# A Mamba block, attention and a mixture of experts on one core: dense products in TensorE's waits behind the scans, and the last queries as three tiles and one

## The chip, the core and the metric

The kernel runs on one core of one Trainium2 chip. A core has five engines that run side by side, each through its own queue in order: TensorE (PE in the profile; its weight loads are PEld) multiplies matrices into PSUM, VectorE (DVE) and ScalarE (ACT) work on tiles, GpSimd (POOL) does a few small operations and here issues the indirect transfers, and SyncE (SP) issues most of the DMA. They wait for each other by semaphores. The metric is the time of one execution on the device, in microseconds (us); the median of several runs counts. In the profile a matmul is shown with the clock that TensorE was granted (PEclk, 1.00 is full speed).

## What is computed

The input is `x` of 4 sequences of 1024 tokens with 128 channels, in float32. Two layers follow each other, each with a residual and a layer norm behind it.

```
# layer 1: a selective state space model, 256 inner channels, 16 states
xz = x @ in_proj_w.T ; xb, z = halves of xz
xb = silu(causal_conv(xb, 4 taps)) ; proj = xb @ x_proj_w.T   # dt_in, B (16), C (16)
dt = softplus(dt_in * dt_w + dt_b)
h[t] = exp(dt[t] * A) * h[t-1] + xb[t] * dt[t] * B[t]         # a scan over 1024 tokens
y = sum over states of h * C + xb * D_param
x = layernorm(x + (layernorm(y) * silu(z)) @ out_w.T)

# layer 2: causal attention (16 heads of 8), then 16 experts, two for each token
n1 = layer_norm(x) ; q, k, v = n1 @ q_w, n1 @ k_w, n1 @ v_w
hidden = x + softmax(causal(q k^T / sqrt(8))) v @ o_w
xt = layer_norm(hidden) ; logits = xt @ router_w
top1, top2 = the two largest ; slot = running count of the expert's tokens before this one
# a token whose slot is beyond the expert's capacity of 512 is dropped for that expert
moe = sum over both experts of gate * 0.8 * fc2(gelu(fc1(xt)))
x = layernorm(x + hidden + moe)
```

A token's place in its expert is a running count over all tokens before it (`cumsum` over the 4096 tokens), so the routing of the last tokens needs the totals of all earlier ones.

## The kernel before

Tokens are worked on in 32 tiles of 128; half a sequence is 512 tokens, four tiles. The program has three stages. First the scans of layer 1 run, half a sequence at a time; VectorE is their engine. Beside them, and behind them for the last sequence, runs attention. Then come the experts: each reads its 512 slots (`xe`, L1462), runs two products and a GELU, and scatters its rows to the tokens (L1492). At the end the two rows of each token are added with their gates.

Attention works on one half sequence of queries at a time (`stream`, L756), in four groups of four heads (`for g in range(NG)`). For each block of 128 keys it makes scores (`pst`, L782), their exponentials on ScalarE (`pr`, L792), and weighted sums (`av`, L804) one block later. Blocks on the diagonal are masked; for the very last half (`e.last`) VectorE does so by a product with a triangle (L795). A group's sums end in `avs` (L843).

The order of the queues of TensorE and VectorE is that of the program text (`manual_schedule` with `pinned` engines), and that text is interleaved by hand: each side task is a generator, cut by `yield` into pieces, and `piece()` (L1566) advances each of its queues by one piece for every key block of attention (`next(attend)`). A `yield USE` marks a piece whose results are used in the first round of the next call, ahead of the scores. The queues are `before` (inputs of the next half: norm, transposes, products of queries and keys, L669), `after` and `final` (what follows a half's weighted sums), `aside` (routing), `loads` (expert weights) and `sending` (transfers of routed rows).

What follows weighted sums: for all halves but the last `rest_of_half` (L854) divides by the sums of the exponentials, which go through DRAM, and projects (L886); `tokens_of_half` (L931) transposes back; `after_projection` (L942) adds the residual, norms the rows (L960), transposes them (L969) and makes the logits (L975) and their copy in `lg` (L980). For the last half `group_of_last` (L890) does it group by group: a product with a selector spreads the sums (L911), a reciprocal and a product on VectorE (L916, L917), the projection (L923) into one bank that all groups add to. Its fourth group is done in two halves of two tiles each (L811 to L845), so that the norm of the first two lies beside the scores of the others; the second goes to `final`.

The norm behind the scans (`pace.first`) takes its inverse root by three Newton steps on VectorE (`inv_std_steps`, L156), four small operations a step.

Routing (`send`, L1259) takes a range of tiles: the largest logit, its place by products with a triangle into `pcum` (L1333), slots, then the same for the second; then each tile's two rows go out by indirect DMA on GpSimd (`transfer`, L1279). Tiles 0 to 15, 16 to 23 and 24 to 27 are sent while attention runs, one transfer after the other; each waits for the one before. The last four tiles are routed when the loop has ended (L1687), and their eight transfers follow each other without such waits. The experts' reads wait for the last group of transfers (`sent[-1]`, L1463). `counted` (L1613) counts the halves that are through, by which the ranges become due (L1682 to L1685).

Of the kernel before, what the change touches and what calls it, by code (L numbers as in the profile page):

```python
# [10 lines left out]
F32 = mybir.dt.float32  # L11
# [3 lines left out]
ALU = mybir.AluOpType  # L15
# [32 lines left out]
NPART, NPAIR = 3, 9  # L48
USE = 1
SCORE_MAX = 40.0  # L50


@with_exitstack
def mamba_then_moe_block_kernel(ctx: ExitStack, tc: tile.TileContext, a: dict, out: bass.AP):
# [101 lines left out]
    def inv_std_steps(pool, var, n, tag):  # L156


        ve = pool.tile([P, n], F32, tag=tag + "_ve", name=tag + "_ve")
        nc.vector.tensor_scalar(ve, var, LN_EPS, None, ALU.add)  # L160
        r = pool.tile([P, n], F32, tag=tag + "_rs", name=tag + "_rs")
        t = pool.tile([P, n], F32, tag=tag + "_nt", name=tag + "_nt")
        nc.vector.tensor_scalar(r.bitcast(I32), ve.bitcast(I32), 1, None, ALU.logical_shift_right)
        nc.vector.tensor_scalar(r.bitcast(I32), r.bitcast(I32), -1.0, float(0x5F3759DF), ALU.mult, ALU.add)
        for _ in range(3):
            nc.vector.tensor_tensor(t, r, r, ALU.mult)
            nc.vector.tensor_tensor(t, t, ve, ALU.mult)
            nc.vector.tensor_scalar(t, t, -0.5, 1.5, ALU.mult, ALU.add)
            nc.vector.tensor_tensor(r, r, t, ALU.mult)
        return r  # L170
# [486 lines left out]
    def attention(ph, weights, last_bank):  # L657
# [98 lines left out]
        def stream(todo, then, rows, after, final):  # L756
# [3 lines left out]
            while True:  # L760
# [8 lines left out]
                for g in range(NG):  # L769
# [40 lines left out]

                    halves = 2 if e.last and g == NG - 1 else 1  # L811
                    n = TPH // halves
                    for i0 in range(0, TPH, n):
                        nkb = TPH * qt + i0 + n
# [29 lines left out]
                        if e.last:  # L844
                            then(group_of_last(e, g, t, rows, i0, n), i0 + n == TPH and g == NG - 1, final if i0 else after)  # L845
                    if not e.last:
                        nc.sync.dma_start(e.sums[4 * g : 4 * g + 4, :], t[HD : P : 32, :])
                if not e.last:
                    then(rest_of_half(e, avs, rows), True)
                todo.popleft()  # L850

        held, HELD = [], 5
# [37 lines left out]
        def group_of_last(e, g, t, rows, i0, n):  # L890
# [28 lines left out]
            if not i0:  # L919
                yield  # L920
            po = zbank("po") if i0 else e.po
            for i in range(i0, i0 + n):
                nc.tensor.matmul(  # L923
                    po[:, i * P : (i + 1) * P], lhsT=t[:, i * P : (i + 1) * P], rhs=wo[:, g, :],
                    start=i0 > 0, stop=i0 > 0 or g == NG - 1 and i == i0 + n - 1,
                )
            if g == NG - 1:
                yield USE
                yield from after_projection(e, po, rows, i0, n, e.hid if i0 else None)
# [12 lines left out]
        def after_projection(e, pt, rows, i0, n, hid=None):  # L942
# [20 lines left out]
            if rows.xrow is None:  # L963
                to_tokens(x2_d, t0, x2)
                rows.stored = t0 + 4
            yield
            pt = zbank("pt_x2")
            for i in range(n):
# [14 lines left out]

        return inputs, stream

# [213 lines left out]
    def routing(ph):  # L1199
# [45 lines left out]

        totals, sent, in_turn = [None, None], [], []

# [10 lines left out]

        def send(t0, n, bank, later=None, staged=False):  # L1259
            ts = slice(t0, t0 + n)  # L1260
# [12 lines left out]

            group = (f"sent{t0}", []) if later is None else None
            earlier = in_turn[-1:]
            if group:
                sent.append(group[1])

            def transfer(i, t, row):  # L1279
                ins = scatter(xin, s.put[i][:, t : t + 1], row, group, earlier)  # L1280
                if group:
                    wait_for(ins, earlier)
                else:
                    in_turn[:] = [ins]
# [37 lines left out]
            def places(m, i, name):  # L1322
# [18 lines left out]
                nc.vector.tensor_reduce(place, loc, AX.X, ALU.add)  # L1341
                total = keep.tile([P, E], F32, tag=f"total{i}_{t0}", name=f"total{i}")
                if totals[i] is None:
# [210 lines left out]
    with tc.If(mild > 0) as cmp:  # L1554

        with ExitStack() as late:
            with ExitStack() as ph:
# [54 lines left out]

                def counted(rest):  # L1613
                    yield from rest
                    finished.append(rest)
                    if len(finished) * TPH == SOON:
                        after.append(send(0, SOON, bank_z, sending.append, staged=True))
# [10 lines left out]
                with ExitStack() as ssm:  # L1628
                    with ExitStack() as first:
# [15 lines left out]
                    last_bank = lambda name: ps_last.tile([P, HL], F32, tag="last", name=name)  # L1645
                    attention_inputs, attention_stream = attention(ph, weights, last_bank)
                    attend = attention_stream(
                        middle, lambda rest, all_, to=after: to.append(counted(rest) if all_ else rest), rows, after, final
                    )
# [18 lines left out]
                def send_early(t0, n):  # L1668
# [122 lines left out]
```

## Time and profile before

| | us |
|---|---|
| three runs | 1239.41, 1233.44, 1253.04 (median 1239.41) |
| the profiled execution | 1231.83, its span 1229.9 |
| mean granted clock of TensorE | 0.848 |
| busy: TensorE, VectorE, ScalarE, GpSimd | 923.8, 880.8, 678.4, 265.2 |
| last weighted sums of the half before the last | 893.5 |
| first scores of the last half | 901.66 |
| routing of the last four tiles | 1032.3 to 1039.5 |
| their transfers on GpSimd | 1036.6 to 1046.4 |
| first expert's transposes | 1050.90 |
| first expert's result on VectorE | 1062.84 |

A line of the timeline has the start, the time that a run of like instructions took, the engine, the line of the program, what it writes from what, the shape, how many, and in brackets how long the engine had stood idle and what ended that. A line of the windows has, for a stretch of time, its length and for each engine the busy time with the number of instructions, then the granted clock, the DMA engines' busy share and GB/s. A busy TensorE in the profile is one with a product in flight; it need not be at its peak. One product of float32 shows as two records.

### The profile page before, as it was taken

Reading aid. Unit: us, or ns where it says so; the run is one execution under the profiler, and the core shown is the slowest. Engines: PE = TensorE matmul, PEld = TensorE weight load, DVE = VectorE, ACT = ScalarE, POOL = GpSimd, SP = SyncE. Lnnn points to the kernel's source line nnn. Section 1 sums busy time; section 2 is a strip of 40 time slices with the busy share of each in tenths; the row PEclk is TensorE's granted clock in tenths of the full one; section 3 lists DMA queues with packets and bytes.
Section 4 is the critical chain, followed back from the end, with each engine's and each line's share of the span. In section 5 each row is a group of like instructions: output and inputs, shape, how many; then the busy total and the mean of one; then the engine's idle time right before and its main releaser. Section 6 shows DMA issues by size and latency. Waiting matters only on the chain. (4 is left out here: it accounts for less than half of the span.)

```text
span 1229.9 us, 15466 instructions
## 1 busy us (share of the span) xinstructions
PE 923.8 (75%) x5388; PEld 442.2 (36%) x5388; DVE 880.8 (72%) x1328; ACT 678.4 (55%) x1006; POOL 265.2 (22%) x248
## 2 busy tenths in 40 slices
PE   4687852267889888889988497987878873789965
PEld 2332310033434334424334233332422332566645
DVE  2199698999899999899999999788543555112205
ACT  1467556235787894577875366575443551823224
POOL 1020012130211001101102213454103202244443
PEclk9989976566999998799989688888956995899997
DMA  3965476616554553542562442133662201522117
GB/s 69 308 245 198 158 268 224 217 65 219 164 172 132 171 163 127 159 144 82 194 181 72 160 149 88 44 115 110 155 191 89 74 12 52 170 67 69 46 36 206
DMA packets 170680, 171.02 MB, mean 139 GB/s; under 512 B 31984, under 2 KB 126144, under 8 KB 170464
## 3 DMA queue, kind: packets, MB, share of 16 engines
q1 hardware_dynamic: 155296, 143.16, 38.5%
q10 hardware_dynamic: 11200, 18.35, 4.1%
q0 software_dynamic: 4096, 8.43, 2.1%
q8 instruction: 44, 0.72, 0.3%
q14 instruction: 44, 0.36, 0.1%
HBM read 110.80 MB, written 59.10 MB: 138 GB/s over the span
## 5 line engine op out<-in xcount | busy, mean ns | idle before, releaser
L792 ACT ACTIVATE pr<-pst 128x1024 f32<-128x1024 f32 (+3 forms) x396 | 292.9, 792 | 121.2 <-PE pst L782 72.0
L536 ACT ACTIVATE da<-dt_sp,a_neg 128x512 f32<-128x512 f32 x256 | 179.0, 722 | 117.9 <-DVE h L542 106.8
L782 PE MATMUL pst<-qst,kst 72*128 72x512 bf16 (+3 forms) x792 | 197.1, 351 | 41.3 <-ACT pr L792 19.9
L804 PE MATMUL av<-pr,vp 128*32 128x512 f32 (+3 forms) x1584 | 181.3, 526 | 2.0 <-DVE pr L795 1.6
L532 DVE TENSOR_TENSOR h<-u_sp,bt 128x2048 f32<-128x2048 f32 x64 | 145.4, 2276 | 16.5 <-DMA u_sp<-u_d 16.5
L542 DVE TENSOR_TENSOR_SCAN h<-da,carry,h 128x512 f32<-128x512 f32 x128 | 155.8, 1265 | 1.7 <-ACT da L536 1.7
L542 DVE TENSOR_TENSOR_SCAN h<-da,h 128x512 f32<-128x512 f32 x128 | 148.4, 1206 | 6.7 <-ACT da L536 6.7
L552 PE MATMUL py<-h,sel 128*32 128x512 f32 x512 | 86.9, 758 | 83.8 <-DVE h L548 55.0
L548 DVE TENSOR_TENSOR h<-h,ct 128x2048 f32<-128x2048 f32 x64 | 146.2, 2285 | 1.1 <-POOL carry L545 0.3
L782 PEld LDWEIGHTS <-kst 72*128 72x128 bf16 x792 | 66.3, 103 | 183.0 <-issue 153.5
L545 POOL COPY carry<-h 128x4 f32<-128x4 f32 x32 | 44.6, 1392 | 355.6 <-DVE h L542 336.9
L1477 ACT ACTIVATE hT<-ph,b 128x512 f32<-128x512 f32 x64 | 43.9, 686 | 80.7 <-PE ph L1476 79.7
L127 POOL DMA_INDIRECT eout<-eo,to x64 | 61.4, 960 | 88.4 <-DVE eo L1488 54.1
L301 PE MATMUL pt_x<-xT,w_tap 128*128 128x512 f32 x128 | 60.8, 631 | 18.2 <-DVE w_tap L283 7.4
L1476 PE MATMUL ph<-xeT,w 128*128 128x512 f32 x128 | 61.9, 619 | 12.9 <-DVE xeT L1472 12.9
L1483 PEld LDWEIGHTS po_e<-w,hT 128*128 128x128 f32 x512 | 61.5, 192 | 13.0 <-issue 12.2
L127 POOL DMA_INDIRECT xin<-row,put x32 | 47.0, 1468 | 77.1 <-issue 29.3
L1483 PE MATMUL po_e<-w,hT 128*128 128x128 f32 x512 | 63.2, 277 | 0.1
L788 PE MATMUL pst<-mask_k,identb 128*128 128x128 bf16 x448 | 62.8, 225 | 0.0
L127 POOL DMA_INDIRECT xin<-xrow,put x32 | 31.1, 971 | 137.5 <-DVE p L1211 45.3
L804 PEld LDWEIGHTS av<-pr,vp 128*32 128x32 f32 x1584 | 36.3, 112 | 60.8 <-issue 37.6
L552 PEld LDWEIGHTS py<-h,sel 128*32 128x32 f32 x512 | 12.3, 119 | 123.4 <-DVE h L548 69.1
(255 smaller groups left out, 1200.5 us busy)
## 6 DMA issues: line engine op xcount, KB each, us to landing
dt_sp<-dt_d SPq DMA_DIRECT2D x64, 256.0 KB
u_sp<-u_d SPq DMA_DIRECT2D x64, 256.0 KB
kst<-k_parts SPq DMA_DIRECT2D x96, 144.0 KB
qst<-q_parts SPq DMA_DIRECT2D x64, 144.0 KB
bt<-bc_d SPq DMA_DIRECT2D x32, 256.0 KB
ct<-bc_d SPq DMA_DIRECT2D x32, 256.0 KB
w<-in_fc_w_dram SPq DMA_DIRECT2D x32, 256.0 KB
xin<-clear SPq DMA_DIRECT2D x8, 516.0 KB
```

The lines of the kernel that those rows point to most:

```text
L127: ins = nc.gpsimd.indirect_dma_start(out=dst[:, :], out_offset=bass.IndirectOffsetOnAxis(ap=rows, axis=0), in_=src, in_offset=None).ins
L532: nc.vector.tensor_tensor(s.h, s.u, four(s.bt), ALU.mult)
L536: nc.scalar.activation(s.da[jl], s.dt[:, jl, :], AF.Exp, scale=a_neg[:, j, s.g : s.g + 1])
L542: ins = nc.vector.tensor_tensor_scan(h, s.da[jl], h, from_, ALU.mult, ALU.add).ins
L548: nc.vector.tensor_tensor(s.h, s.h, four(s.ct), ALU.mult)
L552: nc.tensor.matmul(s.py[jl * NR : (jl + 1) * NR, :], lhsT=sel, rhs=s.h[:, jl, :], start=(s.g == 0), stop=(s.g == NG_S - 1),)
L782: nc.tensor.matmul(pst[:, jj, :w], lhsT=ks[ki // TPH][jp][:, jj, ki % TPH * P : (ki % TPH + 1) * P], rhs=qs[jp][:, jj, q0:c1], start=True, ...
L788: nc.tensor.matmul(pst[:, jj, :P], lhsT=identb, rhs=mask_k, start=False, stop=True)
L792: nc.scalar.activation(pr[:, :, :w], pst[:, :, :w], AF.Exp, scale=QSCALE)
L804: nc.tensor.matmul(av[32 * j : 32 * j + 32, q0 : q0 + w], lhsT=e.vps[ki // TPH][:, ki % TPH, v0 : v0 + 32], rhs=pr[:, jj, :w], start=(ki = ...
L1476: nc.tensor.matmul(phh, lhsT=w1[e][:, c * P : (c + 1) * P], rhs=xeT, start=True, stop=True)
L1483: nc.tensor.matmul(po[:, i, :], lhsT=hT[:, c, i * P : (i + 1) * P], rhs=w2[e][:, c, :], start=(c == 0), stop=(c == NFC - 1),)
```

## The change

It has six parts. (1) A new function `busy(n)` issues `n` products of the identity with itself, 128x512 in float32, into one of the two banks of the scores; nobody reads them. It is called with 7 ahead of the first group of the last half, with 3 and 6 before and behind the last projection of the last tile, and with 2, 1, 2, 2 and 12 behind the pieces of the last routing. (2) The fourth group of the last half is split into three tiles and one, for two and two. (3) `group_of_last` has one more `yield` ahead of the projection, and `after_projection` three more between the norm and the transposes, when the scans are over. (4) A Newton step is three operations for four. (5) `counted` counts tiles, not halves, so the first three tiles of the last half are routed as a range of their own, and the last tile as another; the three tiles' transfers are a group whose members do not wait for each other, and the last tile's two wait for all of that group. (6) The running totals alternate between two buffers for each choice, for one buffer per range.

```diff
+BUSY, BUSY_SUMS, BUSY_NORM = 7, 3, 6
+BUSY_SEND = 2, 1, 2, 2, 12
...
         for _ in range(3):
             nc.vector.tensor_tensor(t, r, r, ALU.mult)
-            nc.vector.tensor_tensor(t, t, ve, ALU.mult)
-            nc.vector.tensor_scalar(t, t, -0.5, 1.5, ALU.mult, ALU.add)
-            nc.vector.tensor_tensor(r, r, t, ALU.mult)
+            nc.vector.scalar_tensor_tensor(t, t, -0.5, ve, ALU.mult, ALU.mult)
+            nc.vector.scalar_tensor_tensor(r, t, 1.5, r, ALU.add, ALU.mult)
...
-                    halves = 2 if e.last and g == NG - 1 else 1
-                    n = TPH // halves
-                    for i0 in range(0, TPH, n):
+                    if e.last and g == 0:
+                        busy(BUSY)
+                    for i0, n in ((0, TPH - 1), (TPH - 1, 1)) if e.last and g == NG - 1 else ((0, TPH),):
...
-                            then(group_of_last(e, g, t, rows, i0, n), i0 + n == TPH and g == NG - 1, final if i0 else after)
+                            then(group_of_last(e, g, t, rows, i0, n), n if g == NG - 1 else 0, final if i0 else after)
...
-                    then(rest_of_half(e, avs, rows), True)
+                    then(rest_of_half(e, avs, rows), TPH)
...
+        def busy(n):
+            pst = ps_s.tile([P, 2, HL], F32, tag="ps_s", name="pst_busy")
+            for i in range(n):
+                nc.tensor.matmul(
+                    pst[:, i % 2, :], lhsT=ident, rhs=ident.unsqueeze(1).to_broadcast([P, HL // P, P]),
+                    start=True, stop=True,
+                )
...
             if not i0:
                 yield
+                yield
+            else:
+                busy(BUSY_SUMS)
             po = zbank("po") if i0 else e.po
             for i in range(i0, i0 + n):
...
+            if i0:
+                busy(BUSY_NORM)
             if g == NG - 1:
                 yield USE
...
             yield
+            if pace.first and not i0:
+                for _ in range(3):
+                    yield
             pt = zbank("pt_x2")
...
-            group = (f"sent{t0}", []) if later is None else None
-            earlier = in_turn[-1:]
+            group = (f"sent{t0}", []) if later is None or free else None
...
             def transfer(i, t, row):
+                earlier = sent[-2] if len(sent) > 1 and later is None else in_turn[-1:]
                 ins = scatter(xin, s.put[i][:, t : t + 1], row, group, earlier)
...
-                total = keep.tile([P, E], F32, tag=f"total{i}_{t0}", name=f"total{i}")
+                tag = f"total{i}_{ranges[i] % 2}"
+                ranges[i] += 1
+                total = keep.tile([P, E], F32, tag=tag, name=f"total{i}")
...
-                def counted(rest):
+                def counted(rest, n):
                     yield from rest
-                    finished.append(rest)
-                    if len(finished) * TPH == SOON:
+                    if not n:
+                        return
+                    finished.append(n)
+                    if sum(finished) == SOON:
...
-                    yield from send(t0, n, bank, sending.append)
+                    last = t0 + n > NT - TPH
+                    yield from send(t0, n, bank_z if last else bank, sending.append, free=last)
...
-                        known = len(finished) * TPH
+                        known = sum(finished)
...
-                for _ in send(early, NT - early, bank):
-                    pass
+                for i, _ in enumerate(send(early, NT - early, bank)):
+                    busy(BUSY_SEND[i])
```

With it the order on TensorE becomes: the transposes and logits of the half before the last behind the last products of queries and keys, then the seven products, then group 0; the transposes and logits of the next half at the sixth and seventh key block of group 1; the products of group 0 (L907, L911, L923) in group 2, together with the routing of tiles 24 to 27; the logits of the three tiles behind the last weighted sums, then the last tile's, then the routing of the three tiles, then that of the last tile, then 14 products ahead of the first expert.

More of the change, by code (lines that the diff above doesn't have):

```diff
@@ L982, in after_projection @@
             )
-        return inputs, stream
+        return inputs, stream, busy
     def attention_with_maxima(ph):
@@ L1244, in rows_of @@
             return s.xrow, s.behind
-        totals, sent, in_turn = [None, None], [], []
+        totals, ranges, sent, in_turn = [None, None], [0, 0], [], []
         def has_slot(t0, n):
@@ L1257, in has_slot, with send @@
             return ok
-        def send(t0, n, bank, later=None, staged=False):
+        def send(t0, n, bank, later=None, staged=False, free=False):
             ts = slice(t0, t0 + n)
@@ L1645, in mamba_then_moe_block_kernel @@
                     last_bank = lambda name: ps_last.tile([P, HL], F32, tag="last", name=name)
-                    attention_inputs, attention_stream = attention(ph, weights, last_bank)
+                    attention_inputs, attention_stream, busy = attention(ph, weights, last_bank)
                     attend = attention_stream(
-                        middle, lambda rest, all_, to=after: to.append(counted(rest) if all_ else rest), rows, after, final
+                        middle, lambda rest, n, to=after: to.append(counted(rest, n)), rows, after, final
                     )
```

## The prediction

> **What bounds the kernel now.** I read the page's slices of the span first, then windows by group of the last queries, one-microsecond windows around each change of the granted clock, the timeline of TensorE, and last the chain of waits. All edits lie behind 880 us, so only the stretch from there to the experts matters.
>
> The slices (31 us each) show TensorE busy while its clock is not full; slices 29 to 35 hold the last queries and the way to the experts:
>
> ```profile
> PE   4687852267889888889988497987878873789965
> PEclk9989976566999998799989688888956995899997
> ```
>
> By group (length, busy time and number of instructions of TensorE, weight loads, VectorE, ScalarE, GpSimd, then granted clock, DMA share, GB/s). The first three lines are groups 0, 1 and 2 of the last queries, then the two halves of group 3, then the way from the last weighted product to the first expert:
>
> ```profile
> 901.66:936.39 34.73, 34.12 (x148) 9.99 (x149) 14.12 (x52) 13.93 (x19) 7.78 (x8) 0.58 0.47 138
> 936.39:971.41 35.02, 27.87 (x142) 10.46 (x141) 17.30 (x64) 14.43 (x19) 8.91 (x9) 0.76 0.29 86
> 971.41:989.22 17.81, 16.38 (x110) 5.40 (x107) 9.55 (x25) 13.35 (x18) 5.76 (x6) 1.00 0.16 49
> 989.22:1001.43 12.21, 9.23 (x84) 4.46 (x82) 5.66 (x6) 6.60 (x13) 0.96 (x1) 1.00 0.03 7
> 1001.43:1020.00 18.57, 14.04 (x110) 6.43 (x108) 8.99 (x31) 9.01 (x18) 0.00 (x0) 0.82 0.02 7
> 1020.00:1050.90 30.90, 5.89 (x33) 4.34 (x33) 15.72 (x82) 9.13 (x30) 7.68 (x8) 0.55 0.25 73
> ```
>
> Groups 0 and 1 take 35 us each at clocks of 0.58 and 0.76, group 2 half of that at 1.00, with the same scores. Why the clock stays low:
>
> ```profile
> 905.00:910.00 5.00, 5.00 (x31) 1.90 (x30) 1.08 (x7) 1.83 (x2) 0.00 (x0) 0.50 0.65 195
> ...
> 930.00:931.00 1.00, 1.00 (x2) 0.48 (x3) 0.00 (x0) 0.00 (x0) 0.51 (x1) 0.50 0.00 0
> 931.00:932.00 1.00, 1.00 (x4) 0.52 (x3) 0.00 (x0) 0.00 (x0) 0.00 (x0) 0.92 0.20 66
> ```
>
> ```profile
> 901.66 1.86 PE L782 MATMUL pst<-qst,kst 72*128 72x512 bf16 x4 [5.31 <-DMA qst<-q_parts]
> ...
> 929.89 4.31 PE L886 MATMUL po<-avs,wo 128*128 128x512 f32 x8
> ...
> 941.94 1.32 PE L969 MATMUL pt_x<-ident,xrow 128*128 128x128 f32 x4 [4.51 <-DVE xrow L196]
> ...
> 955.85 2.08 PE L907 MATMUL po<-ob_diag,ones_f 128*128 128x512 f32 x2
> ```
>
> A wait of 5.31 us precedes the last queries and the clock is 0.50 behind it. It stays there for 29 us of busy scores and weighted sums, and rises 1 to 2 us after full 128x128 float32 products begin (L886 at 929.89, L907 at 955.85). The wait of 4.51 us for the normed rows takes it away again at 941.7. So the scores hold a full clock (959 to 1008) but do not raise a low one.
>
> The end of the stretch, by the chain of waits (start, length, what):
>
> ```profile
> 1044.17 2.49 DMA xin<-xrow,put
> 1046.71 1.13 issue
> 1047.97 2.89 DMA xe<-xin
> 1050.90 1.13 PE pt_xe L1470 x4
> ```
>
> The transfers set the first expert, and from there the chain is TensorE, then scatters at a steady pace: what is won before it shifts the end one for one.
>
> **The change part by part**, against the profiled execution (1231.83 us; span 1229.9, 1.9 around it). The shown median is 1239.41, 7.6 above.
>
> *Seven products before group 0.* One 128x512 float32 product is two records: L1476's eight take 3.70 us at full clock, 0.93 a product; at half L907's starts lie 0.86 apart, 1.72 a product. Seven cost 6.5 to 12.0 us. Cover: the gap from 896.35 to 901.66, 5.3 us. The transposes and logits moved behind `pv` (L969 1.01, L975 1.07) use 2.1 of it. In exchange the queries' product no longer queues behind L969's wait of 3.29 us, but its successors wait for VectorE, which ends the norm only 0.6 us earlier, and ScalarE now runs `x2T` (0.78) and `vp` (0.59) ahead of `mid` of the keys. I take +1 us; ends -3 (the chain moves up by L969's wait) and +8 (all seven at half clock, gap gone). Uncovered they'd cost 12.
>
> *Group 0 at full clock.* Group 2's 17.81 us hold L911 (1.13), L923 (1.16) and 0.98 of wait: 14.5 for the scores alone. Group 0 adds two rounds of `pcum` (1.5 us at half clock, 0.8 full, from the rows at 907.51 and 917.49), four `pr2` (0.4 each) and about 1.3 of waits for VectorE: 19.0, so -15.7. Bounds: -17 (no wait), 0 (the clock stays at 0.50).
>
> *Group 1 and the three extra pieces before the transposes.* The 4.51 us wait goes: VectorE has the rows ready some 13 us into the group, the transposes now stand behind the sixth block of scores. 14.5 + L886 3.6 + L937 0.6 + L969 0.6 + L975 0.8 + 1.2 of waits = 21.3: -13.7; bounds -16 and -4.5 (only the wait goes).
>
> *Group 2 gets what was pushed.* The pieces move back in their queue: L907 and L911 of group 0, both `pcum` rounds of tiles 24 to 27, and L911 of group 1 now all lie in group 2. VectorE's order there: reciprocal 3.36 and product 0.69 (L916 and L917 at 959.15), 22 small operations of routing, masks, reciprocal and product again, 14 more small ones, and only then the mask for the sixth block. At 0.2 to 0.26 us each and 0.4 a mask (two per block), from 3 us into the group: 4.05 + 5.3 + 2.6 (wait for the fifth block) + 0.75 + 4.05 + 2.6 + 2.25 = 21.6, to 24.6; with the last weighted sums 25.5: +7.7. TensorE stands still some 5 us before the sixth block's weighted sums. Bounds +3 (TensorE's own sum: 20.7) and +11 (the clock drops there).
>
> *Group 3 as three tiles and one.* The first part has 7 key blocks of 384 columns for 6 of 256: by ScalarE's exponentials 0.75 a pair for 0.55, 14 us: +2; at half clock +9. The part for one tile is over some 14 us later instead of 18.57, -4.5: its last mask (L795) waits behind the norm of three tiles on VectorE, as L969 did for 3.82 us at 1012.49. The norm loses 3 of 15 steps at 0.2 us; two of four norms are on the path: -1.2. Routing three tiles, then one, runs twice in series: the single batch took 7.3 us (1032.2 to 1039.5), so +8. The last tile has two transfers where there were eight at a pitch of 1.27 us; behind the last `put` 4 x 1.27 us and the queue go, -5.7. But those two wait for all six transfers of the three tiles; those are over while the last tile is routed, and nothing but the experts' scatters queues behind them on GpSimd: +1.5. Three products ahead of the last projection: 2.8 us beside a reciprocal and product of 1.2 (L916's 3.36 and 0.69, a quarter of the columns): +1.5; at half clock +4. Six beside the norm of 4.5 us: +1; the five between routing steps lie under VectorE's 15 or so operations: 0. Sum with the first part: +2.6, bounds -5 and +12.
>
> *The start of the experts.* The last 14 products (13 us full, 24 half) end at most 4 us after the reads arrive, but the first GELU now comes behind 30 copies `by_gate` (0.30 us each), before behind 25: ScalarE hides that. At full clock L1476's first four products take 3.70 instead of 5.93: -2.2, and five more copies +1.5: -1; bounds -3, +8 (14 products at half clock).
>
> The smaller buffers for the totals, the reorder of weight loads on SyncE (queued ahead of none that TensorE waits for) and the stored tail: 0; DMA is at 0.02 to 0.3 from 960 to 1035.
>
> Sum: +1 - 15.7 - 13.7 + 7.7 + 2.6 - 1 = -19.1: 1231.8 - 19.1 = 1212.7. I say 1212, as the execution that stands for the median should lose less to the gate's chance than before's did.
>
> **Rule and row.** The Trainium skill (TensorE: Matmul & The Clock Gate, Part 1: The HAM clock gate) says that some 3.4 us of sustained activity give the full clock, whatever is issued. By it groups 0 and 1 would have warmed by themselves, the added products would only lengthen the queue, and the sum would hold the 4.51 us wait and about 3 us of slow start: some 1224 us. No row here agrees: 29 us of busy scores at 0.50.
>
> **The rivals.** *The clock is lost again in group 2.* The stall of 5 us is as long as those of 3.3, 4.5 and 3.8 us after which the clock fell (886.9, 941.7, 1013). If the scores of group 3 don't raise it, the upper ends of groups 2 and 3's first part hold: +3.3 and +7: 1223. For: each such gap cost the clock. Against: L911 and L923 are dense and come early in group 3.
>
> *It holds everywhere.* Group 2 at TensorE's sum (-4.7), group 3 and the tail at -5 (-7.6), the experts -2: 1198. For: 959 to 1008 held through waits of 2 us.
>
> *Slower: the products don't raise the clock and stand in TensorE's order as work.* Place: the seven before group 0 and the 28 of the tail. Groups 0 and 1 stay as they are but for the 4.51; 35 x 1.72 = 60 us have about 25 of cover (5.3, then 1.2, 4.5, 4 and 10 in the tail), so +35, group 2 +7.7: 1270. It decides if the first scores of group 0 run at 0.50. Against it are L886 and L907, the same shape.
>
> *It doesn't do what it says:* the clock rises, then falls in group 0 at a wait for keys (TensorE waited 1.17 us for `kst` at 920.3). With half of group 0's and 1's gain: 1227.
>
> **How the numbers follow.** Forecast 0.45 (own range 1204 to 1220), holds everywhere 0.28, lost in group 2 0.15, half gain 0.05, slower 0.07. Two per cent, about what a measurement here can tell from no change, is 1214.6 and 1264.2. Two thirds of the forecast's range and the second rival lie below: 0.58, rounded to 0.6; the rest of it with the two small-gain cases 0.33; slower 0.07. The range 1192 to 1232 leaves out the slower case and the extreme of the fastest.
>
> **What would show it.** Clock 1.00 in groups 0 and 1 and each near 20 us: right; 0.50 behind the seven products: the third rival. A gap of about 5 us before the sixth block of group 2 and its length near 25: right; 18 to 20 there: the second. Clock in group 3 tells the first. The forecast is wrong if group 0 stays near 35 us, or if the stretch from the last weighted sum to the first expert grows past 36 us.

## The result, and the profile after

| | before | after |
|---|---|---|
| median of 20 runs | 1243.31 us (1229.72 to 1253.04) | 1241.47 us (1230.36 to 1255.15) |
| ratio to before, 95% interval | | 1.0013 (0.9988 to 1.0037) |
| the profiled execution, its span | 1231.83, 1229.9 us | 1235.43, 1233.6 us |
| mean granted clock | 0.848 | 0.863 |
| busy TensorE | 923.8 us | 949.6 us |

The change gives nothing that can be measured. The ratios, here and below, leave out slow executions (over 1.5 per cent above the fastest of the same kernel) and are not quotients of these medians; the profiles of the split alone and of the base come from such executions, so no stretch of theirs is given. The forecast was 1212, with a range from 1192 to 1232; both the time and the likeliest direction were wrong.

The slices of the changed kernel, TensorE's busy tenths above its granted clock (31 us each):

```profile
PE   4687853267799897799988587877789888888965
PEclk9989886566999988889989688888897888999987
```

Slices 30 and 31 (894 to 956 us) have 0.9 and 0.7 of the clock where before had 0.5 and 0.6, and slice 34 0.8 for 0.5; 32 and 33 fall from 0.9 to 0.8. The windows of the last queries tell more. The columns are as before; the lines are groups 0, 1 and 2, the part of three tiles, the part of one, and the way from the last weighted sum to the first expert:

```profile
909.17:933.58 24.41, 22.41 (x137) 6.30 (x135) 12.93 (x48) 12.94 (x17) 4.88 (x5) 0.76 0.70 209
933.58:956.03 22.45, 21.86 (x125) 8.32 (x121) 9.64 (x37) 14.71 (x19) 6.69 (x6) 0.88 0.45 133
956.03:984.17 28.14, 23.01 (x140) 9.71 (x139) 17.36 (x50) 13.94 (x19) 8.66 (x9) 0.88 0.17 53
984.17:997.62 13.45, 12.44 (x99) 4.91 (x95) 6.51 (x8) 9.70 (x15) 4.09 (x4) 1.00 0.07 21
997.62:1012.11 14.49, 9.70 (x107) 5.52 (x105) 9.02 (x28) 5.66 (x17) 0.00 (x0) 0.83 0.03 8
1012.11:1051.13 39.02, 34.41 (x98) 16.72 (x97) 20.11 (x118) 7.38 (x25) 7.67 (x8) 0.84 0.31 92
```

Against the six lines of before: group 0 is 10.3 us shorter, group 1 12.6, group 2 10.3 longer, the two parts of group 3 1.2 longer and 4.1 shorter, and the last stretch 8.1 longer with 34.4 us of busy TensorE where it had 5.9. The lead-in is 2.7 us shorter, from the start of the last norm's transposes (879.42 before, 889.61 after) to the first scores of group 0. From the first expert's transposes to the end it takes 182.5 us for 179.0. The sum is 6.5 us less, counted from those transposes on. What lies ahead of them is the same code, yet 10.2 us later: the last scan of the states began at 861.4 for 856.0, and in the other profiles below it begins anywhere from 858 to 871.

Where group 0 lost its clock, TensorE's timeline and three windows of five microseconds:

```profile
920.38 0.61 PE L783 MATMUL pst<-qst,kst 72*128 72x512 bf16 x2 [0.71 <-DMA kst<-k_parts]
921.24 0.60 PE L783 MATMUL pst<-qst,kst 72*128 72x512 bf16 x2 [0.26 <-DMA kst<-k_parts]
```

```profile
915.00:920.00 5.00, 4.54 (x40) 1.53 (x38) 2.83 (x14) 3.88 (x4) 1.04 (x1) 1.00 0.90 260
920.00:925.00 5.00, 4.36 (x16) 0.96 (x17) 3.05 (x17) 2.04 (x3) 0.96 (x1) 0.68 1.05 314
925.00:930.00 5.00, 5.00 (x23) 0.94 (x21) 2.92 (x7) 2.60 (x4) 1.29 (x2) 0.50 0.42 134
```

The clock is full until the fifth block's scores wait for their keys, 0.97 us in all. It is 0.50 from 921.8 to 938.9, with TensorE busy throughout. That is the course of the rival that had 0.05.

The end, from the chain of waits (start, length, what):

```profile
1015.85 5.11 PE pst_busy L857 x6
1020.97 0.22 PE po L936 x2
1021.19 5.15 PE pst_busy L857 x12
...
1036.06 2.68 PE pst_busy L857 x6
...
1046.01 5.43 ACT by_gate L1530 x19
1051.57 3.31 ACT by_gate L1530 x11
1054.89 1.28 ACT L1498
1056.19 0.70 ACT hT L1498
```

Products that nobody reads stand three times on this chain. Two of them hold the last projection and the last transposes. The third hardly holds the last tile's running count: VectorE wrote the operand of that count at 1038.4, 0.3 us before the chain leaves the products. At the chain's end are ScalarE's 30 copies and the load of the GELU (L1498 without a tile), not a transfer as in before.

### The profile page after: what moved, and what is told of

It is laid out like the page before. It is cut to its first block, busy times and chain, and to the rows that moved or that the text cites. A ratio compares the mean times of both kernels' runs of the same rounds, so it can differ in the third digit from the quotient of the medians.

```text
span 1233.6 us, 15665 instructions
## 1 busy us (share of the span) xinstructions
PE 949.6 (77%) x5474; PEld 453.2 (37%) x5474; DVE 884.2 (72%) x1354; ACT 679.0 (55%) x1010; POOL 264.4 (21%) x248
## 5 line engine op out<-in xcount | busy, mean ns | idle before, releaser
L783 PE MATMUL pst<-qst,kst 72*128 72x512 bf16 (+3 forms) x796 | 193.7, 345 | 35.1 <-ACT pr L793 18.1
L1498 ACT ACTIVATE hT<-ph,b 128x512 f32<-128x512 f32 x64 | 43.6, 687 | 80.3 <-PE ph L1497 79.6
```

The lines of the kernel that those rows point to most:

```text
L783: nc.tensor.matmul(pst[:, jj, :w], lhsT=ks[ki // TPH][jp][:, jj, ki % TPH * P : (ki % TPH + 1) * P], rhs=qs[jp][:, jj, q0:c1], start=True, ...
```

## Experiments

Each profile is cut at one point: "front" runs from the last norm's transposes (`pt_xn`) to the end of group 2 (ScalarE's copy of its sums), "tail" from there to the end of the program. The ratio is that of the times. All runs but those of the kernel before keep the shorter Newton step and the alternating buffers of the totals; neither was tried by itself.

| run | ratio to before (95%) | front | tail |
|---|---|---|---|
| before; its second profile | 1.0028 (0.9981 to 1.0075) | 109.9; 105.9 | 240.6; 243.0 |
| the change; its second profile | 1.0013 (0.9988 to 1.0037); 0.9974 (0.9898 to 1.0049) | 94.7; 90.0 | 249.3; 248.2 |
| front part alone | 0.9816 (0.9754 to 0.9878) | 95.0 | 235.6 |
| tail part alone | 1.0079 (1.0038 to 1.0121) | 110.1 | 247.8 |
| quiet tail | 0.9882 (0.9821 to 0.9943) | 96.3 | 242.8 |
| no seven | 1.0016 (0.9982 to 1.0051) | 94.8 | 248.5 |
| norm pieces alone | 0.9886 (0.9845 to 0.9927) | 97.7 | 233.8 |
| front part and keys | 0.9854 (0.9791 to 0.9917) | 86.1 | 235.9 |
| split, one routing | 0.9936 (0.9904 to 0.9968) | 104.0 | 237.5 |
| nineteen left out | 0.9983 (0.9946 to 1.0019) | 100.6 | 244.5 |
| pieces, keys, seven | 0.9780 (0.9745 to 0.9815) | 84.0 | 232.9 |
| pieces, keys, no seven | 0.9801 (0.9765 to 0.9836) | 98.0 | 235.4 |
| split alone | 0.9918 (0.9877 to 0.9960) | | |
| the change and keys | 0.9900 (0.9847 to 0.9953) | 95.3 | 250.2 |
| base (pieces, keys, seven again) | 0.9796 (0.9728 to 0.9864) | | |
| base and nine | 0.9851 (0.9801 to 0.9902) | 92.3 | 233.5 |
| base and nineteen | 0.9877 (0.9840 to 0.9915) | 85.5 | 235.6 |
| base and early split | 0.9860 (0.9810 to 0.9910) | 97.8 | 239.6 |

The tail repeats to 1 or 3 us. The front does not, since the clock in it is partly chance. Differences of ratios below carry half-widths added in squares, at 1240 us. For the front part alone and the quiet tail the medians of all runs are 1221.85 and 1229.02 us against 1238.91 for the kernel before, 0.986 and 0.992 of it, where the change has 0.9985.

**Front part alone.** From the changed kernel:

```diff
-BUSY, BUSY_SUMS, BUSY_NORM = 7, 3, 6
-BUSY_SEND = 2, 1, 2, 2, 12
+BUSY, BUSY_SUMS, BUSY_NORM = 7, 0, 0
+BUSY_SEND = 0, 0, 0, 0, 0
...
-((0, TPH - 1), (TPH - 1, 1)) if e.last
+((0, 2), (2, 2)) if e.last
...
-n if g == NG - 1 else 0, final if i0
+TPH if g == NG - 1 and i0 else 0, final if i0
```

> The changed kernel with its tail as before: fourth group as two and two tiles, one routing of the last four tiles with eight transfers, and none of the 28 dense products there. Left of the change: the seven products, the pushed pieces, the shorter Newton step. Theory A (the gain is real and given back): from the transposes of the last norm to the first scores of group 3 the changed profile is 15.4 us shorter than before's (-2.75, -10.3, -12.6, +10.3), and its tail and start of the experts 8.8 us longer; without that tail the whole is 12 to 16 us faster than before, a ratio near 0.988. Theory B (nothing is gained on the whole: the profiled run of before lost more to the clock than its usual run, or the gain was chance): ratio 0.998 to 1.002.

0.9816, some 23 us; the stretch of 350.5 us took 330.6. Theory A holds, with a larger gain than it said: the gain is real, and the tail gives it back. 5 us of it lie in the tail itself (235.6 for 240.6).

**Tail part alone.** `BUSY` is 0, and the added `yield`s are taken out.

> The changed kernel without the seven products and without the four added pieces: left are three tiles and one, two routings, the 28 dense products of the tail, the shorter Newton step. Theory A: the tail alone costs, 5 to 10 us slower than before, ratio 1.004 to 1.008, and the stretch from the last weighted sum to the first expert's transposes near 39 us where before has 30.9. Theory B: ratio 0.998 to 1.002 and that stretch 31 to 35 us.

1.0079. The sign and the time are theory A's. The way to the first expert's transposes was 32.4 us, not 39, since without the pieces the three tiles' transposes and logits came ahead of the last scores; those stretches took the time instead (20.2 and 15.0 us for group 2 and the three tiles, 17.8 and 12.2 before).

**Quiet tail.** The two lines of `BUSY` constants as in the first diff, nothing else.

> The changed kernel with the 28 dense products of the tail left out, all else kept. Theory A1 (they stand in TensorE's order as work): three of them held the last projection 3.5 us, six the last transposes 1.4 us, and the last fourteen the first expert's transposes by some 4 us, the last hidden behind the copies on ScalarE: 3 to 6 us faster than the changed kernel. Theory A2 (the tail's time is the two routings in series and the 30 copies ahead of the first GELU; the products are free, or pay by the clock): same as the changed kernel or up to 3 us slower, the first expert's first products at 0.50.

Against the change 0.0131 +- 0.0066, 16 us +- 8, more than theory A1 asked for. By place the tail is 6.5 us shorter, and the way from the last weighted sum to the first GELU 7.0 (43.96 to 36.98 us). Of these, 3.2 are the last gates, which VectorE has ready that much earlier, and 3.8 are copies on ScalarE: 17 stand ahead of the GELU, where the change has 30. The price of the products is shown; its size by the times is larger than by the profiles.

**No seven.** `BUSY` is 0.

> The changed kernel with the seven products ahead of group 0 left out, all else kept. Theory A: they hold the clock at 1.00 up to the wait for keys at the fifth block; without them the wait for the queries takes the clock, group 0 runs at 0.50 from its start: group 0 near 35 us where it took 24.4, so 8 to 12 us slower than the changed kernel. Rival (the clock is at 1.00 from the products of queries and keys and the seven only fill the wait; what counts is the wait for keys): within 3 us of the changed kernel.

The same as the change, and the same front (94.8 for 94.7). The rival holds: in the change's own place the seven products bring nothing. Without them the clock is lost at the wait for queries, 17 us long; with them at the wait for keys, 17 us long.

```profile
912.33 1.87 PE L783 MATMUL pst<-qst,kst 72*128 72x512 bf16 x4 [5.47 <-DMA qst<-q_parts]
```

**Norm pieces alone.** The front part with `BUSY` 0 and without the added `yield` of `group_of_last`.

> The kernel before with two parts of the change alone: the three added pieces between norm and transposes, and the shorter Newton step. No dense products, two and two tiles, one routing. The run with the whole front part left a ratio of 0.982, and from the transposes of the last norm to the end it took 330.6 us where before took 350.5. Theory P (the pieces do it: they take the transposes out of TensorE's way at both norms, so its waits and the clock that they cost go; seven products and the pushed projection bring nothing): ratio 0.980 to 0.988, that stretch 328 to 336 us. Rival (the pushed projection and the dense products carry half of it): ratio 0.990 to 0.996, stretch 338 to 346 us.

331.4 us in the profile as theory P says, 0.9886 by the times, between the two theories. The three pieces and the shorter Newton step make some 14 of the 23 us, and no dense product is in it; the rest, 9 us +- 9, can't be told from nothing. They also shorten the tail by 7 to 9 us against before: the first half of group 3 no longer puts its transposes in front of scores (L969 waited 3.82 us there).

**Front part and keys.** One load is moved:

```diff
                     ks, qs = loaded.pop((e.b, qt, g))
+                    if e.last and g == 0:
+                        ks.append(k_half(e, g, 1))
```

> The run with the whole front part (seven products, pushed pieces, shorter Newton step; tail as before), and the keys of group 0's second half are loaded ahead of the keys of group 1. Theory K (the prediction's 15.7 us for group 0 failed because the fifth block's scores wait for keys whose buffer comes free only with the fourth block's scores, and that wait takes the clock for five slots of 3.4 us): no wait for keys there, the clock stays at 1.00 through group 0, which takes 19 to 21 us where it took 24.4; 4 to 6 us faster than the front part alone, ratio 0.977. Rival (another wait, or the sparse small products of the routing, takes the clock anyway): group 0 at 23 us or more, ratio 0.980 to 0.984.

In the profile theory K holds: no wait for keys, clock 1.00 from 884.7 to 966.6, lead-in and group 0 in 38.2 us for 44.5. This is group 0:

```profile
917.47:936.39 18.92, 17.27 (x138) 5.95 (x136) 12.36 (x48) 13.05 (x17) 3.58 (x4) 1.00 0.59 166
```

The times (0.9854 for 0.9816) can't show it.

**Split, one routing.** The quiet tail, with `counted` told of all four tiles at once, so that they are routed together.

> The changed kernel without the 28 dense products of the tail and with one routing of the last four tiles behind the last one, with eight transfers; three tiles and one kept, and the front part kept. Between the front part alone (two and two, one routing: 0.982) and the quiet tail (three and one, two routings: 0.988). Theory R (two routings in series and what they put ahead of the first GELU cost what the split brings): like the front part alone or better, ratio 0.978 to 0.983, last weighted sum to first expert near 31 us, and the experts 174 us from the first GELU as there. Theory S (the split itself costs, by seven blocks of 384 columns for six of 256 and a norm of three tiles behind which the last tile's masks wait): ratio 0.987 to 0.990.

The time is worse than either theory (0.9936), with a front that lost 9 us more to the clock. By place the tail is 237.5 us: 1.9 over the front part alone, 5.3 under the quiet tail. So in these profiles the second routing costs more than the split.

**Nineteen left out.** `BUSY_SEND` is all 0, the 3 and 6 stay.

> The changed kernel without the 19 dense products behind the pieces of the last routing; the 3 and 6 around the last projection kept. The quiet tail left a ratio of 0.988, the changed kernel 1.001. Theory A (all products ahead of work cost by place): the 3 and 6 held the last projection and the last transposes 4.9 us, so about 0.993; the first expert's transposes come when their rows arrive. Rival (it is the last 12 alone, 4 us of wait): 0.988 to 0.990.

Neither number was met: 0.9983. To the first GELU it takes 40.5 us, half way between 44.0 with all and 37.0 with none. Each of the two sets costs about 3.5 us there, but not in the same way. The 3 and 6 hold work on TensorE. The 19 do not delay the routing: without them the last gates are ready 34.1 us behind the last weighted sum, with them 33.8. What they change is ScalarE's queue, whose order is not that of the program text: with them 30 copies stand ahead of the GELU, without them 17. First the change, then this run:

```profile
1046.01 8.87 ACT L1530 ACTIVATE by_gate<-ident,gate 128x128 f32<-128x128 f32 x30 [4.26 <-DVE gate L1230]
```

```profile
1046.84 5.07 ACT L1531 ACTIVATE by_gate<-ident,gate 128x128 f32<-128x128 f32 x17 [4.27 <-DVE gate L1231]
```

The same holds in every kernel with two routings: 30 copies in the five profiles with the 19 products, 17 in the four without.

**Pieces, keys, seven; and without the seven.** The norm pieces with the moved load, with `BUSY` 7 and 0.

> The kernel before with the three pieces between norm and transposes, the shorter Newton step, the seven products ahead of group 0, and group 0's second keys loaded ahead of group 1's; the projections not pushed, tail as before. Put together from the stretches of two earlier runs (38.2 up to the end of group 0 with the keys; 19.9, then 26.5, 12.2, 13.1, 29.6 and 178.9 from the pieces alone): 318 us from the transposes of the last norm to the end where before has 350.5, the fastest so far, ratio 0.972 to 0.980. Rival (the pushed projections are needed for group 1 or 2 at this pace): 322 to 328 us, ratio 0.981 to 0.986.

> The run before this one in the list without the seven products. It tells what they are worth when no wait for keys follows. Theory H (they hold the clock over the wait of 5 us for the queries): without them that wait takes the clock, the scores of group 0 run at 0.50 for 10 to 20 us, 8 to 12 us slower than with them. Theory N (the scores get the clock back within a slot or two, or have it anyway): within 4 us of the run with them.

The first is the fastest kernel of all, 0.978 and 316.8 us in its stretch (318 expected). Groups 0 and 1 of it, and group 0 without the seven products:

```profile
905.33:924.16 18.83, 17.26 (x137) 5.95 (x135) 12.28 (x48) 13.05 (x17) 3.96 (x4) 1.00 0.57 170
924.16:944.00 19.84, 19.24 (x122) 7.33 (x120) 9.65 (x37) 14.65 (x19) 5.50 (x7) 1.00 0.53 156
```

```profile
909.75:939.70 29.95, 29.69 (x137) 8.04 (x137) 12.77 (x48) 13.04 (x17) 6.74 (x7) 0.50 0.41 116
```

In these two profiles the seven products are worth 14 us in the front. By the times they are worth 0.0021 +- 0.0050, 3 us +- 6: theory N's number, though the 8 us where theory H begins lie just inside the interval. The profiles are the ends of the draw: the one execution was the fastest of its six, the other the slowest of its six. The profile of the base with nine products, with the same seven, lost the clock at 920 and has 92.3.

**Split alone.** The quiet tail with `BUSY` 0 and without the added `yield`s.

> The kernel before with three tiles and one, the two routings in series and the shorter Newton step, and nothing else of the change: no dense product, no added piece. The tail with its 28 products alone cost 0.8 percent. Theory S (the split and its second routing cost, by more columns and later gates): 3 to 8 us slower than before, ratio 1.002 to 1.007. Theory B (only the dense products cost): ratio 0.995 to 1.001.

0.9918, faster than before and better than both theories. That ratio rests on five of nine runs; over all nine the median is 1241.93 us for 1243.99, so the gain is not sure. The order on TensorE tells what the split does here. First this run, then the change:

```profile
1038.93 0.80 PE L922 MATMUL pr<-avs,sel_sum 128*128 128x128 f32 x2 [0.36 <-ACT avs L844]
1039.52 0.25 PE L1348 MATMUL pcum<-m,tri_b 128*128 128x48 bf16 x1
...
1041.11 0.80 PE L936 MATMUL po<-wo,avs 128*128 128x128 f32 x2 [0.53 <-DVE avs L928]
```

```profile
1020.76 0.42 PE L936 MATMUL po<-wo,avs 128*128 128x128 f32 x2
...
1027.24 0.18 PE L1352 MATMUL pcum<-m,tri_b 128*128 128x48 bf16 x1
```

Without the pieces, the three tiles' running count (`pcum`, 128x48) comes ahead of the last tile's projection (`po`); with them it comes 6.5 us behind it, since the pieces push the three tiles' transposes past the last scores. The tail alone against the split alone is 0.0161 +- 0.0059, 20 us +- 7, for the 28 products (9 us by the medians of all runs).

**The change and keys.**

> The whole change, with group 0's second keys loaded ahead of group 1's and nothing else. If the wait for keys is what kept group 0 from the 19.0 us of the prediction, group 0 and the way to it shorten by 5 to 7 us, and the whole change then reads 0.995 to 0.998 where it read 1.001. Rival (the time won there is lost again behind it, in group 2 or the tail): 1.000 to 1.002.

0.990, better than expected by the times, while the profile shows no gain in the front (95.3), so where the times gained is not shown. In the profile another wait took the place of the keys', and the clock with it:

```profile
926.72 0.58 PE L890 MATMUL pr<-ih,sel_b 48*128 48x512 bf16 x1 [3.10 <-DMA ih<-inv]
```

**Base, nine, nineteen, early split.** The base is the fastest kernel. To it come the 3 and 6 products; the 2, 1, 2, 2 and 12; or the split and two routings, with the three pieces left out in the last half:

```diff
-            if pace.first and not i0:
+            if pace.first and not i0 and not e.last:
```

> The fastest kernel so far once more, unchanged, as the base of this set: pieces between norm and transposes, seven products, keys of group 0 first, shorter Newton step, tail as before. Earlier ratio 0.978 (0.9745 to 0.9815); 0.975 to 0.983 again, and the same stretches behind the last weighted sum (33.7 us to the first GELU).

> The base with the three dense products ahead of the last projection and the six behind it (here the last two tiles' projection), nothing else. Theory A (they stand in TensorE's order as work, at 0.50 behind a wait of VectorE): 3.5 to 7 us slower than the base, the way from the last weighted sum to the first GELU 37 to 41 us. Rival (they only fill VectorE's time, and the clock that they bring pays): within 2 us of the base.

> The base with the 19 dense products behind the pieces of the last routing, nothing else. With one routing of four tiles the reads of the first expert come some 14 us behind the routing, time for 14 products at half clock in 24 us or at full in 13. Theory A (the last end after the rows have arrived): first expert's transposes 1 to 5 us later, 1 to 5 us slower. Rival (hidden, and the first eight products at full clock take 3.7 us where they take 5.9): 0 to 3 us faster.

> The base with three tiles and one and two routings, no dense products in the tail, and without the three pieces in the last half itself. Theory J (split and pieces work against each other: the pieces push the three tiles' transposes and logits behind the last tile's scores, so their routing starts only with the last tile's and runs in series; alone the split gained 0.8 percent): 1 to 6 us faster than the base, 30 to 32 us from the last weighted sum to the first GELU. Rival (it is no gain: TensorE waits 3.8 us for the norm of three tiles in front of the last tile's scores): 0 to 5 us slower.

Base 0.9796; nine +0.0055 +- 0.0085, inconclusive, by place nothing (33.9 us to the first GELU, 33.7 in the first profile of the base's kernel); nineteen +0.0081 +- 0.0078 and 36.7 us, as theory A says; early split +0.0064 +- 0.0084. By place theory J is wrong: the way to the first GELU shrinks to 31.1 us, but the two parts of group 3 grow from 25.3 to 34.0, because TensorE waits for the norm again (3.73 us at 1020.1). The split and the pieces each fill the same hole, and by place the pieces fill it better.

**Both kernels once more.**

> The kernel before, unchanged, for a second profile. In the first it took 350.5 us from the transposes of the last norm to the end, and the transposes came at 879 us where ten other profiles have 885 to 898. If that first profile is usual behind the transposes: 348 to 353 us, transposes at 885 to 895. If it was unlucky there and lucky ahead of them: 340 to 346 us. Ratio 0.997 to 1.003 in any case.

> The changed kernel, unchanged, for a second profile. In the first it took 344.0 us from the transposes of the last norm to the end, 6.5 less than before, but the times show no gain. If that profile is usual: 342 to 346 us, lead-in and group 0 near 44, last weighted sum to first GELU near 44. If the usual run loses more to the clock: 348 to 353 us, with 48 to 52 in the lead-in and group 0. Ratio 0.999 to 1.004.

Before: 348.9 us; the change: 338.2 and lead-in and group 0 at 44.0. The first profiles were usual. So the profiles show 5 to 12 us of gain behind the scans, the times none (at most 1.5 us by the first interval; the second alone would allow 12). A part of it is the draw: the change's two profiled executions were 6 and 11 us faster than the medians of their sets, those of before 12 faster and 5 slower. Two profiles of each can't close the rest; it stays open.

## Why the prediction failed

| term | forecast | measured (first profiles) |
|---|---|---|
| seven products, lead-in | +1 (-3 to +8) | -2.7 |
| group 0 | -15.7 (-17 to 0) | -10.3 |
| group 1 | -13.7 (-16 to -4.5) | -12.6 |
| group 2 | +7.7 (+3 to +11) | +10.3 |
| group 3, three tiles; one tile | +2; -4.5 | +1.2; -4.1 |
| rest of the tail | +5.1 | +8.1 |
| start of the experts | -1 (-3 to +8) | +3.5 |
| sum | -19.1 | -6.5 (of unrounded terms) |

Three steps failed: group 0 at full clock (10.3 us won for 15.7), the tail with the start of the experts (8.7 us lost for 1.6), and the start of the sum. That was one profiled execution, 11.5 us below the median of the 20 runs; from the median the same sum is 1224. The prediction let this offset vanish, as the changed kernel should lose less to the clock; the change's own profiled execution lies 6.0 us below its median.

**The front** was nearly right as a sum and wrong in its cause. Forecast -20.7; by place it is 15.2 us shorter in the first profiles, and the front part alone measured 23 us +- 8, its shorter tail included. The prediction gave 15.7 of it to the seven products, but without them the time is the same, and the pieces between norm and transposes alone give 0.9886. The size of a group at full clock was right: 18.8 us in the fastest kernel, 19.0 forecast. The step that failed here is "Group 0 at full clock": the wait for `kst` that stood under "It doesn't do what it says" was priced, but put at 0.05. It does not take a long wait: 0.97 us did it, in two pieces.

**Group 2** went as told: VectorE's queue of reciprocal, products and small operations stood in front of the masks, and TensorE waited 3.77 us where about 5 were forecast.

```profile
974.65 0.79 PE L783 MATMUL pst<-qst,kst 72*128 72x256 bf16 x4
979.21 1.55 PE L805 MATMUL av<-pr,vp 128*32 128x384 f32 x8 [3.77 <-DVE pr L796]
```

The clock fell twice for one slot of 3.4 us; in the fastest kernel, where it fell once, group 2 took 25.6 us, and 25.5 was forecast.

**The tail** is where the gain went, and where the forecast failed worst. Against before it is 5 to 9 us longer (249.3 and 248.2 us for 240.6 and 243.0), where +1.6 was forecast. The pieces in front would have shortened it: with them in both, the tail of the change takes 248 to 250 us in four profiles (the change twice, without the seven, with the keys) and the old tail 233 to 236 in five (front part alone, norm pieces, front part and keys, and the two with pieces and keys). So the split, the second routing and the products cost 12 to 17 us together; by the times 24 +- 8 (1.0013 against 0.9816), by the medians of all runs 15. The forecast's steps, as the prediction put them:

- "beside a reciprocal and product of 1.2 (...): +1.5", "Six beside the norm of 4.5 us: +1", "the five between routing steps lie under VectorE's 15 or so operations: 0". The three held the projection for 5.1 us at a clock of 0.50, where VectorE was through in 1.6 (at 1017.2): 3.5 lost. The six, at full clock, ended 1.4 us behind the norm. The five cost nothing, as forecast: three of them took 2.7 us of the chain, but beside VectorE's work, and the gates came no earlier without them. The sizes had been taken at full clock, with half as the far end.
- "ScalarE hides that", of the 30 copies. They ran from 1046.0 to 1054.9, the GELU's load behind them to 1056.2, while the first expert's first product was done by 1054. The last 14 products ended 4 us after the first rows were there, as forecast; here the copies were later still, and set the first GELU. The 30 were read rightly, but not that 13 of them stand there only because of the products: without the 19 there are 17, and the GELU comes 3.5 us earlier.
- "Routing three tiles, then one, runs twice in series: (...) +8" was near. VectorE began the three tiles' routing at 1024.9, though their logits were there at 1015.5. That the pieces of the same change put it there was not seen; without them the way from the last weighted sum to the first GELU is 31.1 us (base and early split) for 37.0 (quiet tail).
- "-4.5" for the last part came true, but the pieces give it without the split (13.1 us for 18.5 in the norm pieces alone). It was booked for the wrong part.

**The slower rival** had a mechanism that is half the tail's, products that stand in TensorE's order as work; the other half came by ScalarE's queue. For the lead-in it was wrong: the wait for the queries covers all seven there (19.6 us with them, 19.6 without).

**Rule and row.** The prediction set against the rule that scores "do not raise a low one". Too strong: with no full float32 product since 907, the clock rose at 925.1 in the run without the seven. (Of its two examples, L907 came 2.6 us before the rise, not 1 to 2.)

```profile
922.00:925.00 3.00, 3.00 (x12) 0.43 (x4) 1.13 (x4) 1.25 (x2) 1.12 (x2) 0.50 0.09 28
925.00:930.00 5.00, 4.10 (x39) 1.39 (x38) 2.32 (x14) 1.51 (x3) 1.84 (x2) 0.99 0.74 232
```

Elsewhere they stayed at 0.50 for 29.7 busy us. The Trainium skill (TensorE: Matmul & The Clock Gate, Part 1: The HAM clock gate) says that some 3.4 us of sustained activity suffice. The same section says that the window runs free, so that what is lost varies by run. The second agrees with the runs (84 and 92 us for the same front); the first does not (those 29.7 us).

## What to carry to other kernels

Filling an engine's waits with idle work can pay only where the wait ends by something that does not itself stand behind the filler, and here it paid nothing that the times show even there. Price each filler at the low clock, follow what is queued behind it to the engine that was to cover it, and compare the queues of the engines whose order is not pinned with and without it. Look first for what causes the wait: putting a transpose behind three more blocks of scores, with a shorter Newton step, gave about 1 percent, and in the profile a load of keys moved ahead kept a clock that seven products had not kept. When a change has several parts, ask of each pair whether one pushes away what the other meant to start early.

## What the runs showed of the hardware

The granted clock changes on a grid of 3.41 us: every stretch at 0.50 in these traces is a whole number of such slots, from one (the most frequent) to seventeen, but for the last of each, which the end of the program cuts off. At full clock a slot with little work lost it, but no single share of busy time tells: 2.38 us of scores and weighted sums (973.0 to 976.5 in the change) kept it, 2.44 us with the routing's small products (918.4 to 921.8) lost it. Scores, weighted sums and those small products alone raised it again after three busy slots in one profile (920.0 to 930.2, base and nine) and not in nine in another (909.9 to 940.6 in pieces, keys, no seven). Our reading, which no run tested, is that whether a kernel keeps its clock over a wait of one microsecond depends on where the slots fall. One profile is one draw: the front of two kernels that differ only behind it took 84 and 92 us.
